# Graph network, four layers on one core: layer 3's early products in float32r halves, count matrices finished earlier, layer 4's loads moved

## The chip, the cores and the metric

The kernel runs on one core of one Trainium2 chip, in one launch. A core has a matrix engine (PE, with PEld for its weight loads), a vector engine (DVE), an activation engine (ACT), a general engine (POOL), a sequencer that here only issues transfers (SP), and 16 DMA engines. ACT, SP and POOL issue transfers from their own instruction streams. PE multiplies with a stationary operand of at most 128 x 128, sums in PSUM, eight banks of 128 x 512 float32. The metric is the time of one execution on the device, in microseconds (us); less is better.

## The reference

6250 nodes with 256 features, 100,000 edges sorted by their destination; half of all edges end at the first quarter of the nodes.

```python
h = relu(layernorm(x))
h = sage_mean(h)          # mean over in-edges of h[src]; h @ W_self + mean @ W_neigh + b
h = sage_pool(h)          # hp = relu(h @ W_pool + b_pool); max over in-edges of hp[src]
h = sage_gcn(h)           # (sum over in-edges of h[src] + h) / (deg + 1) @ W_neigh + b
h = sage_mean(h)
return x + (h @ W_fc + b_fc)
```

The hidden width is 512, the output width 256.

## The kernel before

Nodes are worked on in 49 row tiles of 128. The weights of layers 3 and 4 are multiplied together ahead, so layer 3 sums rows of 512 columns and layer 4 rows of 256.

**Sums.** A sum over in-edges is made in two ways. For the first tiles, where the edges are dense, a matrix of edge counts (128 source rows by 128 destination rows, kept in HBM as fp8 in `tab_a`) is multiplied with the table's rows: function `dense`, with `a` the counts as stationary operand and `z` a row tile as moving one. For the others the rows are gathered by edge (`sums`, POOL's `ring` gathers) and multiplied with 0/1 matrices. Layer 1 does so for 8 tiles densely, layer 3 for 18 (`H3`), layer 4 for 22 (`H4`). In layer 3 a float32 row is kept as three bf16 parts (`r3`, 3 x 512 columns in `tab_r`), so one row tile and one destination tile take three bf16 products. [...]

**The pooling layer** (L1650, from 732 to 1901 us). 782 steps of 128 edges: POOL gathers rows `X` (256 KB), DVE makes a running maximum with one and a half operations a step (L1631), SP stores the rows back two steps at a time (L1635). Six `X` tiles are in flight. Work of other layers is laid between the steps, by a counter `at`. `hub` builds the narrow count matrices (functions `build_narrow`, destination tiles 8 to 21, 448 rows `hm` and `ht`): 320 of them up to step `EARLY_AT` = 250 with `hm` made on DVE (L380), and 128 between steps 270 and 640 (`REST`) with `hm` made on ACT (L376 and L378). Row tiles finish in `done2` (one each 13 steps from step `FIRST_AT` = 112 on, when the block of edges that holds them is through; the carries between blocks are the products `ptcf`, `pcf`, and the last tile is `last_done2`). Source tiles 10 to 41 (`EARLY`) are taken for layer 3 as they finish: `early_products` makes batches of four, loads their counts for each of the 18 destination tiles on SP (`ae`, L1601), multiplies (L575) and adds into `acc3` on DVE (`add3`, L1307). `early.advance` spreads what is ready over at most 32 steps. The first 10 tiles' rows stay in SBUF (`kept_rows`) for layer 3; until those tiles finish, its places hold rows of the batches.

**Layer 3** multiplies what is left: the kept rows and tiles 42 to 48, which are read back into `zt` tiles (`resident`). Counts come through `stream`, four pieces ahead on ACT's queue (`ac`). `done3` finishes a tile and stores it.

**Layer 4** keeps some of layer 3's row tiles in SBUF (`z4_kept`, 23 tiles), reads the other 26 back (`z4_late`), and streams counts in the same way, cast three pieces ahead. `load4` loads a tile's input row `xr` and its own part `q` on ACT's queue (L1848, L1850, seven buffers each), DVE adds them (L1864), adds the scaled sum (L1866), and SP stores `out` (L1869). The order written is changed by a scheduler only through what the pools' buffers and the engines allow.

## Time and profile before

| | us |
|---|---|
| median of 3 runs | 2769.23 (2764.82 to 2772.06) |
| the profiled execution | 2768.88 |
| its span in the trace | 2767.1 |

| engine | busy us | share of the span |
|---|---|---|
| PE | 2363.3 | 85% |
| DVE | 2074.8 | 75% |
| POOL | 1881.4 | 68% |
| PEld | 1341.6 | 48% |
| ACT | 1240.6 | 45% |

The mean granted PE clock is 0.936 and the DMA engines move 295 GB/s in the mean. The shares are means over stages with different limits, so the stages are read apart: layer 1 up to 731 us, the pooling layer with its tail up to 1956, layer 3 up to 2390, layer 4 to the end. A row of the profile gives the line, the engine, the operation, what goes out and in, the count, the busy time and the mean ns of one; behind the second bar stands the idle time of the engine before these instructions, and what ended it. A chain is a path of waits followed back from the last instruction; its rows are a start, a duration and a place.

### The profile page before, as it was taken

To read this page: it belongs to the slowest core of one execution; us is meant where nothing else is said; L and a number is where in the kernel's file an instruction comes from. 1 tells how busy PE (TensorE), PEld (TensorE's weight loads), DVE (VectorE), ACT (ScalarE), POOL (GpSimd) and SP (SyncE) were. 2 spreads that over 40 slices of the span, in tenths; PEclk is the share of its full clock that TensorE was granted. 3 is DMA by queue.
4 is the path that set the end of the run, shared out by engine and by line. 5 is a ranking of instruction groups with operands and counts; after the bars stand their busy time and mean duration, and the time that the engine had idled before them with its cause. 6 is when DMAs were issued, how large, how long until landed. Compare 5 with 4: busy or idle time off the path is not lost.

```text
span 2767.1 us, 38367 instructions
## 1 busy us (share of the span) xinstructions
PE 2363.3 (85%) x10823; PEld 1341.6 (48%) x10913; DVE 2074.8 (75%) x5438; ACT 1240.6 (45%) x2833; POOL 1881.4 (68%) x2193
## 2 busy tenths in 40 slices
PE   3688999999686565788899998799899999798897
PEld 2356666767443222343344443344344444476676
DVE  8888777766699898788788897774376777466666
ACT  5467777763388887753444343211000000244333
POOL 5477777777566676777667776663477777577675
PEclk8799999999897687899999999999999999899999
DMA  8567777777799999999999999895799999999897
GB/s 273 154 183 204 208 210 212 223 228 222 243 362 334 309 351 318 331 347 345 315 307 331 342 357 298 296 311 189 280 370 382 379 391 388 328 344 308 284 302 225
DMA packets 360123, 815.18 MB, mean 295 GB/s; under 512 B 58798, under 2 KB 149014, under 8 KB 359868
## 3 DMA queue, kind: packets, MB, share of 16 engines
q0 software_dynamic: 145168, 511.30, 56.6%
q1 hardware_dynamic: 142248, 211.90, 21.1%
q10 hardware_dynamic: 72484, 89.43, 9.5%
q8 instruction: 89, 1.46, 0.2%
q14 instruction: 134, 1.10, 0.1%
HBM read 607.75 MB, written 205.46 MB: 294 GB/s over the span
## 4 chain that ended last, share of the span: by engine, by line
PE 45%; DMA 27%; DVE 14%; issue 5%; ACT 3%; POOL 2%; ACTq 0%; DVEq 0%; POOLq 0%
PE pd L575 14%; PE pg L516 11%; DMA X<-rows,srcIf 9%; DVE run L1631 5%; PE pd L569 4%; DMA ring<-tab_h,srcT 4%; DMA rows<-X 4%; PE pm_hp L1176 3%; DMA xr<-in_x 2%; DVE X L1631 2%; PE pm_prf L1548 2%; PE pm_hp L1170 2%; PE pb L346 2%; POOL X L1650 2%; DVE acc L547 1%
## 5 line engine op out<-in xcount | busy, mean ns | idle before, releaser
L1650 POOL DMA_INDIRECT X<-rows,srcIf x782 | 742.6, 950 | 346.6 <-issue 147.5
L1631 DVE SCALAR_TENSOR_TENSOR run<-run,samef,X 128x512 f32<-128x512 f32 x758 | 572.4, 755 | 65.3 <-DMA X<-rows,srcIf 59.6
L495 POOL DMA_INDIRECT ring<-tab_h,srcT x474 | 456.3, 963 | 148.9 <-issue 53.4
L516 PE MATMUL pg<-ring,hot 128*128 128x256 bf16 (+2 forms) x2342 | 492.1, 317 | 45.7 <-DMA ring<-tab_h,srcT 33.5
L575 PE MATMUL pd<-kept_rows,ae 128*128 128x512 bf16 x1520 | 395.0, 393 | 61.2 <-DVE acc L1307 48.2
L495 POOL DMA_INDIRECT ring<-tab_r,srcE x314 | 317.4, 1011 | 126.6 <-issue 49.4
L547 DVE SCALAR_TENSOR_TENSOR acc<-pg,M,acc 128x256 f32<-128x256 f32 (+2 forms) x629 | 322.8, 540 | 76.6 <-PE pg L516 72.5
L569 PE MATMUL pd<-zt,af 128*128 128x512 f32 x1078 | 305.8, 406 | 46.9 <-ACT af L1750 40.1
L516 PEld LDWEIGHTS <-hot 128*128 128x128 bf16 x2364 | 230.7, 98 | 233.2 <-issue 88.0
L495 POOL DMA_INDIRECT ring<-tab_s,srcE x266 | 254.4, 956 | 122.7 <-PE pg L513 48.7
L1631 DVE SCALAR_TENSOR_TENSOR X<-X,samef,run 128x512 f32<-128x512 f32 x379 | 282.2, 744 | 53.8 <-DMA X<-rows,srcIf 35.0
L575 PEld LDWEIGHTS <-ae 128*128 128x128 fp8e4 x1728 | 171.8, 100 | 305.3 <-issue 156.7
L569 PEld LDWEIGHTS pd<-zt,af 128*128 128x128 f32 x1078 | 208.0, 195 | 104.8 <-ACT af L1750 44.4
L1750 ACT CAST af<-ac 128x896 fp32r<-128x896 fp8e4 (+2 forms) x176 | 146.6, 846 | 217.5 <-PE pd L569 53.8
L491 DVE TENSOR_SCALAR hot<-iota_bf,keyE 128x128 bf16<-128x128 bf16 (+1 forms) x580 | 152.9, 284 | 107.8 <-PE pg L516 75.4
L1548 PE MATMUL pm_prf<-unf,hTf 128*128 128x512 f32 x384 | 197.4, 641 | 3.3 <-ACT hTf L1538 3.3
L401 ACT ACTIVATE A<-pb 128x392 fp8e4<-128x392 f32 x224 | 109.3, 499 | 191.2 <-PE pb L396 177.9
L338 ACT ACTIVATE hs<-ht,onef 128x128 bf16<-128x128 bf16 x396 | 153.5, 393 | 88.7 <-PE pb L346 87.7
L575 PE MATMUL pd<-Z,A 128*128 128x256 bf16 (+1 forms) x1176 | 184.6, 274 | 0.7 <-ACT A L351 0.6
L372 ACT ACTIVATE ht<-iota_bf,skR 128x128 bf16<-128x128 bf16 x448 | 155.9, 400 | 13.3 <-DMA col<-in_L_gnn_b 9.4
L337 ACT ACTIVATE ht<-iota_bf,sk 128x128 bf16<-128x128 bf16 x396 | 153.1, 398 | 8.3
L340 DVE TENSOR_SCALAR hm<-iota_w,mk 128x392 bf16<-128x392 f16 x461 | 150.5, 334 | 5.1 <-PE pb L346 4.8
(378 smaller groups left out, 3794.5 us busy)
## 6 DMA issues: line engine op xcount, KB each, us to landing
rows<-X SPq DMA_DIRECT2D x385, 256.0 KB
tab_r<-kept_rows ACTq DMA_DIRECT2D x44, 384.0 KB
ac<-tab_a ACTq DMA_DIRECT2D x128, 112.0 KB
rows<-hpf SPq DMA_DIRECT2D x49, 256.0 KB
th<-tab_t ACTq DMA_DIRECT2D x49, 256.0 KB
X<-rows,srcIf POOLq DMA_INDIRECT x782
tab_a<-A ACTq DMA_DIRECT2D x14, 784.0 KB
tab_t<-th SPq DMA_DIRECT2D x37, 256.0 KB
```

The source lines that it names most:

```text
L337: nc.scalar.activation(t, iota_b, AF.Abs, bias=sk[:, r : r + 1])
L338: nc.scalar.activation(hots[0], t, AF.Relu, bias=one, scale=-1.0)
L372: nc.scalar.activation(held["ht"][:, i, :], iota_b, AF.Abs, bias=sk[:, r : r + 1])
L491: nc.vector.tensor_scalar(hot[j], iota_b, keyT[:, j - jb : j - jb + 1], None, op0=ALU.is_equal)
L495: nc.gpsimd.indirect_dma_start(out=ring[:, j % deep, :].bitcast(F32) if wide else ring[:, j % deep, :], out_offset=None, in_=table, in_off ...
L516: mm = nc.tensor.matmul(pg[:, : F + c], hot[j], X[:, part * F : (part + 1) * F + c], start=(k == 0 and part == 2), stop=(k == n - 1 and pa ...
L547: nc.vector.scalar_tensor_tensor(acc[d], half, m, acc[d], op0=ALU.mult, op1=ALU.add)
L569: nc.tensor.matmul(hold[0], a, z, start=(s == ss[0]), stop=(s == ss[-1]))
L575: nc.tensor.matmul(hold[0][:, : F + c], a, z[:, part * F : (part + 1) * F + c], start=(s == ss[0] and part == 2 and s != own), stop=(s == ...
L1548: nc.tensor.matmul(pm, hT[:, c, :], un[:, c, :], start=False, stop=(c == KH - 1))
L1631: nc.vector.scalar_tensor_tensor(put, held, st, row, op0=ALU.mult, op1=ALU.max)
L1650: nc.gpsimd.indirect_dma_start(out=X[:, k, :], out_offset=None, in_=tab_p, in_offset=bass.IndirectOffsetOnAxis(ap=srcI[:, t : t + 1], axis=0),
```

## The change

(a) The early products take two float32r halves in place of three bf16 parts, for source tiles 8 to 39 in place of 10 to 41; the counts are cast on ACT (`aw`). `done2` makes the halves (two ACT copies and two products with `minus_r` and `ident_r`) ahead of the three parts, which still go to HBM. (b) All 448 narrow rows are built by step 310 with `hm` on DVE; early products begin behind step 320. (c) In layer 3 eight kept rows are halves, nine tiles are resident, and counts come in four pieces per tile. (d) In layer 4 twelve tiles are kept and 37 read back; counts are loaded nine pieces ahead, casts two ahead with four buffers; `load4` issues on SP.

```diff
-EARLY = (10, 42)
+EARLY = (8, 40)
-EARLY_AT = 250
-REST = (270, 640)
+EARLY_AT = 310
...
-                if late:
-                    t = pool.tile([P, NT * WIN2], BF16, name="hd", bufs=2)
-                    nc.scalar.activation(t, iota_w[:, : NT * WIN2], AF.Abs, bias=mk[:, r : r + 1],
-                                         scale=-1.0)
-                    nc.scalar.activation(hm, t, AF.Relu, bias=one, scale=-1.0)
-                else:
-                    nc.vector.tensor_scalar(hm, iota_w[:, : NT * WIN2], mk[:, r : r + 1], None,
-                                            op0=ALU.is_equal)
+                nc.vector.tensor_scalar(hm, iota_w[:, : NT * WIN2], mk[:, r : r + 1], None,
+                                        op0=ALU.is_equal)
...
-            for part in () if wide else (2, 0, 1):
+            order = () if wide else (1, 0) if s in halved else (2, 0, 1)
+            for part in order:
...
+            if d < EARLY[1]:
+                r2 = row_parts(d)
+                top_, rest_ = r2[:, :FH], r2[:, FH:]
+                nc.scalar.copy(top_, pm)
...
+                    nc.tensor.matmul(pm, minus_r, top_, start=False, stop=True, skip_group_check=True)
...
+                nc.scalar.copy(rest_, pm)
...
+                    nc.tensor.matmul(pm, ident_r, top_, start=False, stop=True, skip_group_check=True)
...
+        def widened(got):
+            if 1 not in got:
+                got[1] = early_pool[0].tile([P, BATCH, P], F32R, name="aw", bufs=4)
+                nc.scalar.copy(got[1], got[0])
...
-                    got[0] = early_pool[0].tile([P, BATCH, P], F8, name="ae", bufs=16)
+                    got[0] = early_pool[0].tile([P, BATCH, P], F8, name="ae", bufs=14)
...
+                    if i >= 2:
+                        widened(loaded[i - 2])
...
+                    if at == EARLY_AT + 8:
+                        while copies:
+                            copies.pop(0)()
+                        side.close()
+                        early_pool.append(side.enter_context(
+                            tc.tile_pool(name="early3", bufs=1, side="right")))
...
-                    early.advance(early.done + math.ceil(
-                        early.left() / max(1, min(32, T - 24 - at))))
+                    if at > EARLY_AT + 10:
+                        early.advance(early.done + math.ceil(
+                            early.left() / max(1, min(32, T - 24 - at))))
...
-            got[i] = pool.tile([P, 7, P], F8, name="ac", bufs=5)
+            got[i] = pool.tile([P, 7, P], F8, name="ac", bufs=deep + 1)
...
-                wide[i] = wide_pool.tile([P, 7, P], F32R, name="af", bufs=5)
+                wide[i] = wide_pool.tile([P, most_wide, P], F32R, name="af", bufs=4)
...
-        z4_kept = ((20, 27), (27, 34), (34, 41), (41, 43))
-        z4_late = ((0, 7), (7, 14), (14, 20), (43, NT))
+        z4_kept = ((31, 37), (37, 43))
+        z4_late = ((0, 7), (7, 14), (14, 20), (20, 26), (26, 31), (43, NT))
...
-            late = ((0, 5), (5, KEPT), (EARLY[1], NT))
+            late = ((0, 4), (4, KEPT), (EARLY[1], 45), (45, NT))
...
-                nc.scalar.dma_start(xr[:n, :], x[d * P : d * P + n, :])
+                nc.sync.dma_start(xr[:n, :], x[d * P : d * P + n, :])
...
-                nc.scalar.dma_start(q[:n, :], xq[d * P : d * P + n, :])
+                nc.sync.dma_start(q[:n, :], xq[d * P : d * P + n, :])
...
-                           wk)
+                           wk, deep=9)
```

DVE at the end of the pooling layer, before: `X2` and `run` are the pooling steps, `acc3` the sums of early products, `segf` and `cTf` the carry of block 1, which waits for PE's `ptcf`.

```order
L1631 SCALAR_TENSOR_TENSOR X2_21026<-run_20668,samef_140,X2_21026 128x512 [waits DMAHW3_49,DMASW5_49,DVE_49]
L1631 SCALAR_TENSOR_TENSOR X2_21026<-X2_21026,samef_140 128x512 [waits DMASW6_49,DVE_49]
L1307 TENSOR_TENSOR acc3_14_10829<-acc3_14_10829,pd_20618 128x512 [waits PE_49]
L1398 SCALAR_TENSOR_TENSOR segf_20726<-keepTf_10856,ptcf_20663 128x128 [waits PE_49]
L1398 SCALAR_TENSOR_TENSOR segf_20741<-keepTf_10856,ptcf_20663 128x128
...
L1307 TENSOR_TENSOR acc3_15_10830<-acc3_15_10830,pd_20659 128x512 [waits PE_49]
L1307 TENSOR_TENSOR acc3_16_10831<-acc3_16_10831,pd_20695 128x512 [waits PE_49]
L1307 TENSOR_TENSOR acc3_17_10832<-acc3_17_10832,pd_20752 128x512 [waits PE_49]
L1426 TENSOR_TENSOR fixf_20781<-fixf_20781,pcf_20815 128x512 [waits PE_49]
```

And with the change, the same place up to the end of the steps; `ptcf_20698` is block 0's own carry, which comes last.

```order
L1669 SCALAR_TENSOR_TENSOR run_20198<-run_20198,samef_144,X2_20548 128x512
L1306 TENSOR_TENSOR acc3_17_10835<-acc3_17_10835,pd_20539 128x512 [waits PE_49]
L1669 SCALAR_TENSOR_TENSOR run_20198<-run_20198,samef_144,X2_20561 128x512 [waits DMASW0_49,DVE_49]
...
L1669 SCALAR_TENSOR_TENSOR run_20198<-run_20198,samef_144,X2_20685 128x512
L1669 SCALAR_TENSOR_TENSOR X2_20692<-run_20198,samef_144,X2_20692 128x512 [waits DMAHW2_49,DMASW0_49,DVE_49]
L1669 SCALAR_TENSOR_TENSOR X2_20692<-X2_20692,samef_144 128x512 [waits DMASW1_49,DVE_49]
L1400 SCALAR_TENSOR_TENSOR segf_20706<-keepTf_10859,ptcf_20698 128x128 [waits PE_49]
L1400 SCALAR_TENSOR_TENSOR segf_20710<-keepTf_10859,ptcf_20698 128x128
L1404 TENSOR_TENSOR cTf_20705<-segf_20706,contTf_10860 128x128 [waits DVE_49]
L1404 TENSOR_TENSOR cTf_20705<-segf_20710,contTf_10860 128x128 [waits DVE_49]
```

The sums `acc3_15` to `acc3_17` and block 1's carry, which stood behind the last step, have moved ahead of it: the last sum has 37 rows of steps behind it, and the last step is followed by block 0's carry at once.

PE in one batch of early products, before: `pd` is the sum, `ae` the fp8 counts, each row tile taking three products with a weight load each (the rows in between are other tiles' work).

```order
L575 MATMUL pd_17459<-kept_rows_10833,ae_17290 128x512
L575 LDWEIGHTS ae_17290
L575 MATMUL pd_17459<-kept_rows_10833,ae_17290 128x512
L396 LDWEIGHTS hs_17082
L396 MATMUL pb_17502<-hm_16963,hs_17082 128x196 [waits PE_49]
L575 LDWEIGHTS ae_17290
L575 MATMUL pd_17459<-kept_rows_10833,ae_17290 128x512
L575 LDWEIGHTS ae_17290
L575 MATMUL pd_17459<-kept_rows_10833,ae_17290 128x512
L575 LDWEIGHTS ae_17290
L575 MATMUL pd_17459<-kept_rows_10833,ae_17290 128x512
```

And with the change, with `aw` the cast counts and `r2` the halves of a tile that is not kept (a weight load is not a row of its own here).

```order
L574 MATMUL pd_18806<-kept_rows_12092,aw_18758 128x512 x4
L574 MATMUL pd_18806<-r2_8_18001,aw_18758 128x512 x2
L574 MATMUL pd_18838<-kept_rows_12092,aw_18780 128x512 [waits DVE_49]
L574 MATMUL pd_18838<-kept_rows_12092,aw_18780 128x512
L1552 MATMUL pm_prf_18841<-usA_10852,th2_18724 128x512 [waits DMAHW2_49,Activation_49]
L1552 MATMUL pm_prf_18841<-usA_10852,th2_18724 128x512
L574 MATMUL pd_18838<-kept_rows_12092,aw_18780 128x512 x4
L1555 MATMUL pm_prf_18841<-usB_10853,th2_18724 128x512 x2
L574 MATMUL pd_18838<-r2_8_18001,aw_18780 128x512 x2
```

Each row tile takes two products where it took three, and other tiles' work still stands between them.

SP in the middle of layer 4, before: only output stores.

```order
L1869 DMA out_0<-xr4_26006 128x256 [waits DMAHW1_49,DVE_49]
L1869 DMA out_0<-xr4_25936 128x256 [waits DMAHW0_49,DVE_49]
L1869 DMA out_0<-xr4_26169 128x256 [waits DMAHW7_49,DVE_49]
L1869 DMA out_0<-xr4_26099 128x256 [waits DMAHW3_49,DVE_49]
L1869 DMA out_0<-xr4_26332 128x256 [waits DMAHW6_49,DVE_49]
L1869 DMA out_0<-xr4_26212 128x256 [waits DMAHW1_49,DVE_49]
L1869 DMA out_0<-xr4_26375 128x256 [waits DMAHW2_49,DVE_49]
L1869 DMA out_0<-xr4_26506 128x256 [waits DMAHW6_49,DVE_49]
```

And with the change, the same stores with the loads of `xr4` and `q4` (each `DMAHW` name is a lane of transfers whose landing is waited for).

```order
L1895 DMA q4_26269<-xq_70 128x256 [waits DMAHW2_49,DVE_49]
L1914 DMA out_0<-xr4_25350 128x256 [waits DMAHW4_49,DVE_49]
L1893 DMA xr4_25826<-in_x 128x256 [waits DMAHW6_49,DMAHW4_49]
L1914 DMA out_0<-xr4_25275 128x256 [waits DMAHW0_49,DVE_49]
L1893 DMA xr4_25842<-in_x 128x256 [waits DMAHW2_49,DMAHW0_49]
L1895 DMA q4_26324<-xq_70 128x256 [waits DMAHW3_49,DVE_49]
L1895 DMA q4_26388<-xq_70 128x256 [waits DMAHW5_49,DVE_49]
L1914 DMA out_0<-xr4_25509 128x256 [waits DMAHW2_49,DVE_49]
L1893 DMA xr4_25989<-in_x 128x256 [waits DMAHW4_49,DMAHW2_49]
L1914 DMA out_0<-xr4_25385 128x256 [waits DMAHW6_49,DVE_49]
```

The loads stand between the stores. The lane that a store takes is also waited for by the `xr4` load right behind it (`DMAHW4_49`, `DMAHW0_49`, `DMAHW2_49`, `DMAHW6_49`), and the `q4` loads wait for DVE.

More of the change, by code (lines that the diff above doesn't have):

```diff
@@ L557, in sums, with dense @@
         del todo[:]
-    def dense(ss, block, rows, F, psd, done, extra=0, wide=False, own=None):
+    def dense(ss, block, rows, F, psd, done, extra=0, wide=False, own=None, halved=()):
         hold = {}
@@ L1446, in row_parts @@
             i = d % ROWS3
+            assert early.done >= over.get(d + ROWS3, 0)
             if i < KEPT:
-                return kept_rows[:, i, :]
-            return early_pool[0].tile([P, 3 * FH], BF16, name=f"r3_{i}", bufs=1)
+                return kept_rows[0][:, i, :]
+            return early_pool[0].tile([P, 2 * FH], F32R, name=f"r2_{i}", bufs=1)
         def last_done2(d):
@@ L1623, in fast_path @@
         copies = []
-        first, rest = (
-            [w for d in ds for w in build_narrow(d, (skR, mkR, RB1), wk, banks, copies, d >= H3)]
-            for ds, banks in ((range(H1, H3), psb), (range(H3, H4), pst))
-        )
+        first = [w for d in range(H1, H4)
+                 for w in build_narrow(d, (skR, mkR, RB1), npool, psb, copies)]
         hub = Hub(first, 12)
-        more = Hub(rest, 12)
         def step(put, held, st, row):
@@ L1756, in stream @@
             widened(1)
-            widened(2)
         def block(d, s):
```

107 lines of the change are left out of this document (69 added, 38 removed).

## The prediction

> **What bounds the kernel now.** I read the busy time by stage first, to see which engine is near its limit in each stage that the change touches. The cuts are: 800 to 1085 us and 1200 to 1896 us (the pooling layer, before and after most count matrices are built), 1896 to 1956 (its tail), 1956 to 2390 (layer 3), 2390 to 2440 (start of layer 4), 2440 to 2767 (the rest of layer 4). The last three columns are the granted TensorE clock, the share of the DMA engines' time, and GB/s.
>
> ```profile
> core 0: us, PE busy (x) PEld busy (x) DVE busy (x) ACT busy (x) POOL busy (x), PEclk, DMA share, GB/s
> 800.00:1085.00 285.00, 185.18 (x601) 88.25 (x599) 262.41 (x713) 242.00 (x558) 197.53 (x208) 0.80 0.96 335
> ...
> 1200.00:1896.00 696.00, 618.78 (x2369) 287.75 (x2412) 571.30 (x841) 249.51 (x544) 472.01 (x499) 0.95 0.95 322
> 1896.00:1956.00 60.00, 56.93 (x193) 27.57 (x195) 17.40 (x50) 14.13 (x25) 4.07 (x5) 1.00 0.30 100
> 1956.00:2390.00 434.00, 414.52 (x1871) 187.59 (x1909) 299.45 (x693) 22.80 (x55) 319.18 (x316) 0.99 0.99 372
> 2390.00:2440.00 50.00, 35.01 (x133) 26.99 (x132) 12.68 (x40) 15.89 (x19) 30.05 (x33) 0.84 1.02 363
> 2440.00:2767.00 327.00, 291.36 (x1210) 230.51 (x1208) 205.21 (x633) 127.78 (x154) 222.53 (x233) 0.96 0.89 290
> ```
>
> Early in the pooling DVE is the bound (262 of 285 us). Later no engine is alone: PE 89%, DVE 82%, DMA 0.95. The tail is PE alone, with DMA at 0.30. Layer 3 has PE at 96% and DMA at 0.99 together. Layer 4 has PE at 89% with DMA at 0.89.
>
> Second, I read the pooling pace from the same windows, for the gather alone (each is one step of 128 edges, the number behind x):
>
> ```profile
> 1191.00:1896.00 705.00, 443.88 (x469) 0.95 0.95 323
> ...
> 1200.00:1240.00 40.00, 27.69 (x30) 1.00 0.98 347
> 1520.00:1560.00 40.00, 28.36 (x31) 0.96 0.99 342
> 1600.00:1640.00 40.00, 28.35 (x31) 1.00 0.99 345
> 1720.00:1760.00 40.00, 23.61 (x25) 1.00 0.88 281
> 1840.00:1880.00 40.00, 23.24 (x25) 0.93 0.88 281
> ```
>
> The late part makes a step in 705 / 469 = 1.503 us. Where the DMA share is 0.98 or more, it makes 30 to 31 steps in 40 us, about 1.31 us each; where the share falls to 0.88, it makes 25 (1.60 us) while PE has a full clock. So something other than DMA holds the slow stretches. Third, the waits there, of SP (which stores the rows and loads the early count blocks in one queue) and of the others, in us and times:
>
> ```profile
> SPq L1601 <- PE pd L575: 33.6, 33, 3.5
> ...
> POOL X L1650 <- DVE run L1631: 56.7, 78, 4.0
> DVE run L1631 <- DMA X<-rows,srcIf: 55.8, 42, 6.8
> ```
>
> SP stands 33.6 us behind early products before it may load the next count block, and the stores of pooled rows stand behind it.
>
> **The tail.** Fourth, the pooling's last operation on DVE (duration min/median/max in ns, then first and last start), and the chain of waits around it (start, us, what):
>
> ```profile
> L1631 DVE SCALAR_TENSOR_TENSOR X<-X,samef x1: 752/752/752, 1901.4 to 1901.4; 128x512 f32<-128x512 f32 x1
> ...
> 1902.30 0.44 PE ptcf L1385 x4
> ...
> 1941.74 0.44 PE pt_hTf L1469 x4
> 1942.18 0.45 PE ptcf L1385 x4
> ...
> 1953.33 0.59 ACT kept_rows L1499
> ...
> 1953.97 0.39 PE pm_last L1503
> ...
> 1956.84 20.18 DMA zt<-tab_r
> ```
>
> DVE's last pooling operation starts at 1901.4, yet block 0's carry products (ptcf) run on PE only at 1942.18: PE works off a backlog for 40 us. From there the last tile needs 14.7 us to 1956.84. In the changed order the sum of the last early product stands ahead of the last pooling steps on DVE, and after block 0's carry PE has some 28 rows, all of the last two tiles. So the 40 us go, and 5 us of backlog may stay. The last tile now makes f32r halves behind its three bf16 parts: two copies on ACT and three matmuls. One copy and one product of this kind take 0.59 and 0.39 us in these rows, so I put 3 us on it. Tail: -40 + 5 + 3, about **-30** (range -18 to -36).
>
> **The late pooling.** The groups that the change touches, with the mean ns of one:
>
> ```profile
> L575 PE MATMUL pd<-kept_rows,ae 128*128 128x512 bf16 x1520 | 395.0, 393 | 61.2 <-DVE acc L1307 48.2 <-ACT acc L1310 9.6 <-DMA rows<-X 0.9
> L569 PE MATMUL pd<-zt,af 128*128 128x512 f32 x1078 | 305.8, 406 | 46.9 <-ACT af L1750 40.1 <-DMA zt<-tab_s 6.7
> L569 PEld LDWEIGHTS pd<-zt,af 128*128 128x128 f32 x1078 | 208.0, 195 | 104.8 <-ACT af L1750 44.4 <-issue 14.4
> L575 PEld LDWEIGHTS <-ae 128*128 128x128 fp8e4 x1728 | 171.8, 100 | 305.3 <-issue 156.7 <-DMA rows<-X 1.8 <-DMA th<-tab_t 0.2
> ...
> 1863.78 2.10 PE L575 MATMUL pd<-kept_rows,ae 128*128 128x512 bf16 x9
> 2428.70 2.43 PE L569 MATMUL pd<-zt,af 128*128 128x512 f32 x10
> ...
> L575 PEld LDWEIGHTS <-ae 128*128 128x128 fp8e4 x1592 | 157.8, 100 | 277.6 <-issue 138.9 <-DMA rows<-X 1.8 <-DMA th<-tab_t 0.2
> ```
>
> Nine bf16 products in a row take 2.10 us, so one each (2.10 - 0.39) / 8 = 0.214 us; ten f32r products take 2.43, so (2.43 - 0.41) / 9 = 0.225 us. The new form costs the same per product, and there are 2 in place of 3. The last row is the window 1200 to 1896 alone: 1592 of the 1728 products lie in it. They leave (341 us), and all 1152 + 36 of the new kind come in (267 us), with two more products in each of some 33 row tiles that finish there (15 us): PE falls from 619 to about 560 us, 1.19 us a step against 1.32. The 128 late builds leave as well. PE is then no bound at 1.31 us a step, the pace at full DMA share; DVE, at 571 / 469 = 1.22 us of work a step, nearly is. SP's count loads wait for a cast on ACT, which is idle for two thirds of this stage, and no longer for PE. If all of it went to the pace of 1.31, 469 steps would save 90 us; if the X loop itself (gather, DVE, store) sets the slow stretches, 0. I take a little under half, **-40** (0 to -70), since the X loop's waits of 57 and 56 us remain.
>
> The Trainium skill, page "TensorE: Matmul & The Clock Gate", section on Fast Weight Load, says the fast load is for inputs that are not FP32, which speaks against float32r counts. The trace agrees on the load (195 against 100 ns) and shows that it is hidden behind the product before it; were the 95 ns not hidden, 1188 of them would be 113 us more on PE, 1.43 us a step, and the saving of this part could be 30 us at most, the sum below -19.
>
> **The early pooling.** All 448 narrow rows are built by step 310, where 320 were by step 250: 448 / 294 = 1.52 a step against 1.37. On DVE a comparison is
>
> ```profile
> L380 DVE TENSOR_SCALAR hm<-iota_w,mkR 128x196 bf16<-128x196 f16 x320 | 74.6, 281 | 19.5 <-PE pb L396 19.4
> L401 ACT ACTIVATE A<-pb 128x392 fp8e4<-128x392 f32 x224 | 109.3, 499 | 191.2 <-PE pb L396 177.9 <-DMA th<-tab_t 8.2 <-DMA rows<-X 4.5
> ```
>
> so 0.15 x 0.281 x 294 = 12 us more on the bound engine, if its own pace holds; ACT (85% busy) also gets a tenth more. Against it the early products no longer begin there, which takes PE work out. I take **+8** (0 to +30), and **+3** for the change of pools at step 318 (0 to +10), where the new products can begin only when the last copies of the builder have left.
>
> **Layer 3.** 8 kept rows for 18 destination tiles lose one product each: 144 x 0.214 = 31 us less PE. The DMA share is 0.99 and the bytes stay, so only a part shows: **-8** (0 to -25). The 36 casts go to ACT, busy 23 of 434 us.
>
> **Layer 4.** At its start 37 row tiles are read back in place of 26: 11 x 256 KB = 2.9 MB at the 363 GB/s of that stretch is **+8** (+3 to +12). Then comes the step I trust least. The xr and q loads move from ACT's queue to SP's, behind the output stores. With seven buffers each xr load waits until the store just ahead of it has landed. On ACT that wait held up casts; on SP it holds up the next store, and the q loads behind it wait for DVE's additions. The chain and waits of before:
>
> ```profile
> 2596.67 4.07 DMA out<-xr
> ...
> 2600.80 4.19 DMA xr<-in_x
> ...
> 2605.08 0.42 DVE xr L1864
> ...
> L1869 SPq DMA_DIRECT2D out<-xr x47: 298/332/914, 2449.5 to 2761.2; - x47
> ...
> DVE xr L1864 <- DMA xr<-in_x: 99.1, 27, 5.7
> PEld pd L569 <- ACT af L1750: 35.2, 22, 5.6
> PE pd L569 <- ACT af L1750: 25.9, 21, 5.1
> ```
>
> A store takes 4.13 us until the load behind it starts, the load 4.28 us until DVE adds. Today 46 intervals between stores fill 311.7 us: 13.55 us for a pair of tiles (one summed by gathers, one by count products). In the new order a pair is a ring: store, 4.13, load; trigger 0.33; second store, 4.13, load; 4.28; DVE's addition, then 7 to 11 DVE rows (0.324 us each, 205.21 / 633) to the next tile's finish: 2.3 to 3.6. Together 15.2 to 16.5 us, 1.6 to 2.9 us over today's pair; for 22 pairs +35 to +64. Against it: ACT is free of these waits, and PE's 36 us of idle in this stage, most of it waiting for casts (25.9 us, and 35.2 of its loads), is what counts nine pieces ahead could save at most. I take **+30** (-30 to +64), near the ring's lower end, since the trace shows both of its legs.
>
> The Trainium skill, page "DMA: Bandwidth & Descriptors", section "Anatomy of one DMA", gives about 2 us and the bytes at 436 GB/s; an estimate from it for 128 KB is 2.3 us, and a ring of 10 us. The trace has 4.07 and 4.19, so the rows decide; with the page's price the ring would bind nothing, and that is the second rival.
>
> **The sum.** -30 - 40 + 8 + 3 - 8 + 8 + 30 = -29 against the profiled execution's 2768.9 us (span 2767.1), which lies 0.4 below the median of 2769.2. Forecast: 2740 us.
>
> **Rivals.** (1) Slower: the ring on SP sets layer 4 at its full +64 and the pooling is held by its X loop, -15: -29 + 34 + 25 = +30, 2799 us. For it speak the DVE waits of 99.1 us for xr, against it that ACT no longer stalls. With the pooling at -15 it decides from 15.5 us a pair. Chance 0.12. (2) The ring does not bind, because its transfers land sooner or the stores come early; layer 4's loop is 0: 2710 us. For it: DMA is at 0.89 there, against it the two rows above. Chance 0.24. (3) The slow stretches of the pooling are the X loop's own, its gain 0, all else as forecast: 2780 us. For it: the 57 and 56 us of waits between X's gathers and DVE; against it SP's 33.6. Chance 0.16. (4) The f32r loads are not hidden among other products: 1188 x 0.195 = 232 us on PE, 792 us for 469 steps that take 705 today, so +87 in place of -40: -29 + 127 = +98, 2867 us; the row of ten speaks against it. Chance 0.02. (5) The ring at its full +64 gives back what pooling and tail save as forecast: -29 + 34 = +5, 2774 us, no change. Chance 0.06. The forecast's own case (2715 to 2765) has 0.40.
>
> **How the numbers follow.** About 0.3% (8 us) is what a measurement of this kernel can tell from no change: 2761 to 2777. Faster: rival 2 (0.24) and nearly all of the forecast's case (0.38): 0.62. Same: 0.02 of it, rival 5, and 0.07 of rival 3, whose 2780 lies at the edge: 0.15. Slower: rivals 1, 4 and the rest of 3: 0.23. The range runs from 2690 (rival 2 with the pooling at -60) to 2795, just short of rival 1's middle: it leaves out half of rival 1, rival 4, the lower part of rival 2 and some of the rest, about 2 in 10.
>
> **What would show it.** Right: block 0's ptcf within 10 us of the last pooling operation; under 1.45 us a gather from step 320 on; a PE product of `aw` 0.22 us behind the last; in layer 4 stores in pairs 15 to 16 us apart, with DVE's addition waiting for xr. Wrong: gathers still at 1.5 us with PE under 80%; an early part over 20 us longer; PE or DVE gaps in layer 4 that go, or that exceed 64 us in sum.

## The result and the profile after

The kernel is slower: 2785.8 us median (2779.1 to 2790.9) against 2769.5, ratio 1.0059 with the 95% interval 1.0034 to 1.0085. The forecast of 2740 us was wrong in its sign; the stated range, 2690 to 2795, still holds the result. The profiled execution has a span of 2777.2 us against 2767.1, so 10.1 us of the 16 can be looked for in the two traces. First the stages of the changed kernel (columns as before: PE, PEld, DVE, ACT, POOL, then the granted clock, the DMA share and GB/s), cut where its own stages end.

```profile
800.00:1085.00 285.00, 176.11 (x585) 84.80 (x584) 262.84 (x703) 246.47 (x568) 199.33 (x209) 0.77 0.95 333
...
1916.00:1940.00 24.00, 16.08 (x46) 7.91 (x47) 7.58 (x21) 4.93 (x9) 0.94 (x1) 0.77 0.45 141
1940.00:2362.00 422.00, 393.40 (x1710) 189.38 (x1745) 290.93 (x688) 41.89 (x85) 314.94 (x314) 0.98 1.00 380
2362.00:2420.00 58.00, 35.44 (x96) 24.63 (x94) 18.19 (x57) 11.99 (x15) 36.94 (x39) 0.74 0.93 341
2420.00:2777.00 357.00, 309.08 (x1252) 242.97 (x1250) 204.50 (x629) 137.17 (x163) 217.22 (x227) 0.94 0.85 270
```

The tail has shrunk from 60 us to 24, and layer 4 has lost DMA share (0.85 against 0.89). Cut at the first gathers of layers 3 and 4 in both kernels, layer 3 has some 16 us less PE (408 to 393) in nearly the same time. Where the stages begin and end is read from the first and last starts of the gathers (`X` in the pooling, `tab_r` in layer 3, `tab_s` in layer 4) and of the output stores, of before (first four rows) and after (last four):

```profile
L1650 POOL DMA_INDIRECT X<-rows,srcIf x782: 940/946/1386, 731.7 to 1895.4; - x196
L495 POOL DMA_INDIRECT ring<-tab_r,srcE x314: 940/946/1724, 1960.3 to 2373.3; - x157
L495 POOL DMA_INDIRECT ring<-tab_s,srcE x266: 940/946/1207, 2387.9 to 2750.8; - x133
L1869 SPq DMA_DIRECT2D out<-xr x49: 298/332/914, 2431.7 to 2761.2; - x49
```

```profile
L1688 POOL DMA_INDIRECT X<-rows,srcIf x782: 940/946/1462, 732.7 to 1914.0; - x196
L492 POOL DMA_INDIRECT ring<-tab_r,srcE x314: 942/946/1723, 1941.9 to 2354.6; - x157
L492 POOL DMA_INDIRECT ring<-tab_s,srcE x266: 940/946/1340, 2367.8 to 2759.6; - x133
L1914 SPq DMA_DIRECT2D out<-xr x49: 263/338/741, 2431.2 to 2770.5; - x49
```

| stretch | before | after | difference | forecast |
|---|---|---|---|---|
| start to the first pooling gather | 731.7 | 732.7 | +1.0 | 0 |
| first to last pooling gather | 1163.7 | 1181.3 | +17.6 | -29 |
| last gather to layer 3's first gather | 64.9 | 27.9 | -37.0 | -30 |
| to layer 4's first gather | 427.6 | 425.9 | -1.7 | -8 |
| to the first output store | 43.8 | 63.4 | +19.6 | +8 |
| to the end of the span | 335.4 | 346.0 | +10.6 | +30 |
| sum | 2767.1 | 2777.2 | +10.1 | -29 |

The forecast of the second row is +8, +3 and -40. Tail, layer 3 and layer 4 in sum (-8.5) came out near their forecast of 0, in part by luck, since the misses of the rows (-7, +6, +12 and -19) nearly cancel. The pooling did not: counted by gathers started, and read to about 1 us, its first 320 steps took 5 us longer, and steps 320 to 781 took 708.7 us against 696, where 656 had been forecast.

```profile
1199.00:1895.00 696.00, 618.78 (x2368) 287.73 (x2412) 572.23 (x843) 249.51 (x544) 472.01 (x499) 0.95 0.95 323
```

```profile
1205.00:1913.00 708.00, 618.41 (x2113) 380.08 (x2132) 590.27 (x907) 265.42 (x494) 475.05 (x503) 0.93 0.95 325
```

The first row is of before, the second of after, over the same steps: PE has the same 618 us of work in both, though 560 had been forecast, the share of DMA is the same, and PE's clock is a little lower. The loss does not lie evenly in these steps: steps 350 to 400 took 77.9 us against 67.1, steps 400 to 781 took 589.4 against 587.6. Steps 350 to 400 of before, then of after:

```profile
1241.00:1308.00 67.00, 54.70 (x209) 24.91 (x212) 59.80 (x86) 20.37 (x48) 50.02 (x54) 0.90 0.98 343
```

```profile
1247.00:1325.00 78.00, 59.42 (x194) 34.48 (x194) 55.85 (x89) 42.88 (x86) 51.11 (x55) 0.84 0.98 341
```

The DMA share is 0.98 in both, at nearly one rate: some 3.6 MB more (78 us at 341 GB/s against 67 at 343) took the 11 us.

### The profile page after: what moved, and what is told of

Same layout as the page of the kernel before. It is cut to its first block, busy times and chain, and to the rows that moved or that the text cites. A ratio compares the mean times of both kernels' runs of the same rounds, so it can differ in the third digit from the quotient of the medians.

```text
span 2777.2 us, 37443 instructions
## 1 busy us (share of the span) xinstructions
PE 2299.6 (83%) x10201; PEld 1418.2 (51%) x10256; DVE 2092.7 (75%) x5568; ACT 1287.6 (46%) x2837; POOL 1877.5 (68%) x2193
## 4 chain that ended last, share of the span: by engine, by line
PE 42%; DMA 32%; DVE 11%; issue 5%; ACT 4%; POOL 3%; ACTq 0%; SPq 0%; DVEq 0%; POOLq 0%
PE pd L574 13%; PE pg L513 9%; DMA X<-rows,srcIf 8%; DMA ring<-tab_r,srcE 5%; DMA ring<-tab_h,srcT 4%; DVE run L1669 3%; DMA out<-xr 3%; PE pm_hp L1175 3%; PE pm_prf L1558 2%; DMA xr<-in_x 2%; PE pm_w L277 2%; PE pm_hp L1169 2%; DMA rows<-X 2%; DMA zt<-tab_s 2%; PE pb L349 2%
## 5 line engine op out<-in xcount | busy, mean ns | idle before, releaser
L1794 ACT CAST af<-ac 128x768 fp32r<-128x768 fp8e4 (+3 forms) x212 | 171.0, 808 | 435.5 <-DMA ac<-tab_a 175.1
L513 PEld LDWEIGHTS <-hot 128*128 128x128 bf16 x2364 | 220.8, 98 | 261.2 <-issue 127.3
L574 PE MATMUL pd<-kept_rows,aw 128*128 128x512 f32 x828 | 259.6, 438 | 11.1 <-ACT aw L1624 5.6
L566 PEld LDWEIGHTS pd<-zt,af 128*128 128x128 f32 x1078 | 215.2, 201 | 86.8 <-ACT af L1794 23.9
L488 DVE TENSOR_SCALAR hot<-iota_bf,keyE 128x128 bf16<-128x128 bf16 (+1 forms) x580 | 147.2, 279 | 97.7 <-PE pg L513 52.0
L1558 PE MATMUL pm_prf<-unf,hTf 128*128 128x512 f32 x384 | 204.3, 659 | 1.9 <-ACT hTf L1548 1.3
L574 PEld LDWEIGHTS pd<-kept_rows,aw 128*128 128x128 f32 x828 | 157.7, 193 | 73.3 <-issue 29.8
L1624 ACT CAST aw<-ae 128x512 fp32r<-128x512 fp8e4 x144 | 89.3, 621 | 161.3 <-PE pd L574 142.8
L488 DVE TENSOR_SCALAR hot<-iota_bf,keyT 128x128 bf16<-128x128 bf16 x474 | 125.4, 274 | 39.5 <-PE pg L513 38.4
```

The source lines that it names most:

```text
L488: nc.vector.tensor_scalar(hot[j], iota_b, keyT[:, j - jb : j - jb + 1], None, op0=ALU.is_equal)
L513: mm = nc.tensor.matmul(pg[:, : F + c], hot[j], X[:, part * F : (part + 1) * F + c], start=(k == 0 and part == 2), stop=(k == n - 1 and pa ...
L566: nc.tensor.matmul(hold[0], a, z, start=(s == ss[0]), stop=(s == ss[-1]))
L574: nc.tensor.matmul(hold[0][:, : F + c], a, z[:, part * F : (part + 1) * F + c], start=(first and s != own), stop=(s == ss[-1] and part == ...
L1558: nc.tensor.matmul(pm, hT[:, c, :], un[:, c, :], start=False, stop=(c == KH - 1))
L1794: nc.scalar.copy(wide[i][:, :n, :], got[i][:, :n, :])
```

## The experiments

Each group ran on one chip, with the kernel before in the same rounds. The groups differ: before took 2763 and 2764 us in the second and third, as in the result, but 3186, 3152 and 3184 us in the first, fourth and fifth, where transfers are slower (272 to 280 GB/s in steps 320 to 781, against 325). The chips' numbers on record are 0, 11, 1, 8 and 1: the third and the fifth group have the same number, so it is not shown that the chip itself makes the difference. Below, a fast group is one with 2763 or 2764 us for before, a slow one the others. Ratios to before, and stretches within one group, are compared; where a stretch is held against another group, the text says so.

**Loads on ACT again, and the three other runs of the first group.** e1 is the changed kernel with

```diff
-                nc.sync.dma_start(xr[:n, :], x[d * P : d * P + n, :])
+                nc.scalar.dma_start(xr[:n, :], x[d * P : d * P + n, :])
```

and the same for `q`.

> The changed kernel with the xr and q loads of layer 4 back on ACT's queue, all else as changed. Theory (the ring on SP): the stretch from the first output store to the end, 346 us with the change and 318 before, comes back to 318 to 325, and the time to about 2760 us (2753 to 2766). Rival (what costs in layer 4 is the 11 tiles read back more, the shorter run of casts and the deeper loads on ACT): the stretch stays over 338 and the time over 2778 us.

Measured 1.0003 of before (0.9981 to 1.0025), with 353.4 us from the first store to the end. The 318 us that the theory gives for before is short: from the first store it is 335.4 us. Without the changed kernel in this group, this decides nothing; it is repeated below.

e2 multiplies one half only:

```diff
-            order = () if wide else (1, 0) if s in halved else (2, 0, 1)
+            order = () if wide else (0,) if once else (1, 0) if s in halved else (2, 0, 1)
...
-                             lambda v, d=d: summed.append((d, v)), own=d, halved=ss)
+                             lambda v, d=d: summed.append((d, v)), own=d, halved=ss, once=True)
```

> The changed kernel with only one of the two halves multiplied in the early products (the other half's products are left out): 594 products fewer, at 0.233 us each 138 us less PE between step 320 and the end of the pooling. Theory (PE bounds that stretch, since the work of the tail now lies in it): steps 350 to 782, 674 us with the change, shrink by 40 us or more, the time to 2745 us or less. Rival (gathers, DVE and row stores set their own pace): under 12 us less, the time over 2774 us.

Measured 0.9932 (0.9908 to 0.9956). Steps 320 to 781 took 812 us against 835 in e1, whose pooling is that of the changed kernel: 23 us less for some 138 us of PE work. Neither theory's number: PE holds a part of the pace, a sixth of what was taken away. In e4 of this group, whose pooling is that of before, the same steps took 809 us, so the change lost some 25 us here, and only 3 of them in steps 350 to 400.

e3 loads the early counts on ACT:

```diff
-                    nc.sync.dma_start(got[0][:, : len(ss), :].bitcast(BF16),
+                    nc.scalar.dma_start(got[0][:, : len(ss), :].bitcast(BF16),
```

> The changed kernel with the early count blocks loaded on ACT's queue, so that SP's row stores no longer stand behind a load that waits for a cast (98.9 us of such waits on SP with the change). Theory (these waits hold the pooling): steps 350 to 782 take 15 to 30 us less, the time 2756 to 2771 us. Rival (PE sets it, and SP's waits lie beside it): within 6 us of the changed kernel, 2780 to 2792 us; ACT has 144 triggers of 0.33 us more, which it has room for.

Measured 0.9956 (0.9929 to 0.9984), steps 320 to 781 in 837 us against 835. Steps 350 to 400 took 15 us less than in e1 (78.7 against 94.1), and the steps behind them 17 us more. In sum the waits of SP lie beside the work, as the rival has it; against e1 the whole time is not clearly different.

e4 is the kernel before with the two loads on SP, the edit of the change itself (`nc.scalar` to `nc.sync` in `load4`).

> The kernel before with only the xr and q loads of layer 4 moved to SP's queue. Theory (the ring on SP): +20 to +30 us, about 2795 us, with output stores in pairs 15 to 16 us apart. Rival (the ring costs only together with the later rows of the change): within 8 us of the kernel before, 2762 to 2778 us.

Measured 1.0019 (0.9990 to 1.0048), some 7 us, with an interval that holds 0 and 15: the theory's 20 to 30 are excluded in this group, and the rival fits.

**The changed kernel as a mark** (c0, no edit). The second group is fast, like that of the result.

> The changed kernel itself, as the mark for the other runs of this group, since a group's chip may differ from that of the result. All theories expect its first result again: 1.003 to 1.009 of the kernel before.

Measured 1.0059 (1.0046 to 1.0072), 2780.2 us: the result again.

**No read-back of 11 tiles** (e5).

```diff
+            Z4.update({s: Z4[s + 11] for s in range(20, 31)})
             for s0, s1 in z4_late:
-                Z4.update(resident(wk, tab_s, FO, s0, s1))
+                if s0 not in (20, 26):
+                    Z4.update(resident(wk, tab_s, FO, s0, s1))
```

> The changed kernel with row tiles 20 to 30 of layer 4 not read back (their products use other tiles' rows that are in SBUF, so the same work with wrong values): 2.9 MB less at the start of layer 4. Theory (the read-back shares the transfers with the gathers that are in flight, which is why the time from layer 4's first gather to its first output store grew from 43.8 to 63.4 us): 12 to 22 us less than the changed kernel, all of it before the first output store. Rival (the read-back runs at the full 363 to 380 GB/s): 8 us less or under. Second rival (the first stores are late because of the xr and q loads on SP's queue behind the read-back): under 3 us.

Measured 1.0048 (1.0032 to 1.0063), 2.5 us under the mark, the intervals overlapping. The first store came 49.3 us after layer 4's first gather in place of 65.8, as the theory said; but the rest took 361.2 us in place of 347.3, so the 12 to 22 us of the whole were missed. A gain at the start was taken back by what follows.

**One count block for all early products** (e7).

```diff
+        one_ae = []
...
-                    got[0] = early_pool[0].tile([P, BATCH, P], F8, name="ae", bufs=14)
-                    nc.sync.dma_start(got[0][:, : len(ss), :].bitcast(BF16),
-                                      tab_a[d, :, ss[0] : ss[-1] + 1, :])
+                    if not one_ae:
+                        one_ae.append(early_pool[0].tile([P, BATCH, P], F8, name="ae", bufs=1))
+                        nc.sync.dma_start(one_ae[0][:, :, :].bitcast(BF16), tab_a[0, :, 0:BATCH, :])
+                    got[0] = one_ae[0]
```

> The changed kernel with the 144 count blocks of the early products replaced by one block, loaded once and used for all (wrong counts, the same casts and products): 9.4 MB less traffic and no count loads between SP's row stores. Theory (the early products' bulk is set by PE, and their start by the burst of count loads): 5 to 15 us less than the changed kernel in steps 320 to 782, mostly in steps 350 to 400. Rival (transfers bound the whole stretch, DMA share 0.95): 28 us less or more, by 9.4 MB at 335 GB/s. Second rival (PE alone): under 4 us.

Measured 1.0046 (1.0028 to 1.0064), 4 us under the mark in the median; in the profile steps 320 to 781 took 696.7 us against 708.7, 9 of the 12 us in steps 350 to 400, as expected. Steps 350 to 400 took 68.4 us, near the 67.1 of before. There the changed kernel shows the burst of count loads with which the early products begin (waits between 1280 and 1325 us: the sum in us, times, the longest):

```profile
ACT aw L1624 <- DMA ae<-tab_a: 12.3, 2, 11.3
POOL X L1688 <- DMA rows<-X: 9.9, 4, 7.1
DVE run L1669 <- DMA X<-rows,srcIf: 9.6, 3, 7.4
```

A cast waits 11.3 us at once for its count block, and gathers and stores of `X` land late at the same time.

**Loads on ACT, beside the mark** (e8). The edit is that of e1.

> The changed kernel with layer 4's xr and q loads on ACT's queue, beside the changed kernel itself on the same chip. Theory (the ring of stores and loads on SP costs the 10.6 us by which the stretch from the first store to the end grew): 8 to 20 us less than the changed kernel. Rival (the ring runs beside PE's work and the stretch grew because fewer tiles are kept): within 4 us of the changed kernel, or up to 8 us more from casts that wait behind loads on ACT.

Measured 0.9993 (0.9980 to 1.0007), 2761.4 us: 19 us under the mark. The stretch from the first store to the end fell from 347.3 to 326.4 us. So where the loads are issued decides, and the theory holds in this group. What stands on SP is seen in the changed kernel's chain in layer 4 (start, us, what), and in SP's waits between 2420 and 2777:

```profile
2606.39 4.07 DMA out<-xr
2610.48 0.33 SPq L1893
...
2610.90 4.04 DMA out<-xr
...
2615.01 3.34 DMA xr<-in_x
...
2618.37 0.42 DVE xr L1909
```

```profile
SPq L1893 <- DMA out<-xr: 111.1, 38, 4.6
SPq L1914 <- DVE xr L1911: 66.5, 24, 8.4
SPq L1895 <- DVE hot L488: 60.0, 17, 5.2
```

A store, its landing, the load behind it, the second store, its landing, the second load, then DVE: the ring that the prediction drew, with 111 us of waits for landings. From a store to the second store behind it the median is 15.5 us, against 13.6 before; 15 to 16 had been named as the sign.

**A tile of its own for the result** (e9). The last operation of layer 4 writes to a new tile, so that a load of `xr` waits for DVE's reading and not for the store:

```diff
+                o = wk.tile([P, FO], F32, name="o4", bufs=6)
...
-                    nc.vector.scalar_tensor_tensor(xr[:n, :], acc[:n, c : c + FO],
+                    last = c + FO >= acc.shape[1]
+                    nc.vector.scalar_tensor_tensor((o if last else xr)[:n, :], acc[:n, c : c + FO],
...
-                nc.sync.dma_start(out[d * P : d * P + n, :], xr[:n, :])
+                nc.sync.dma_start(out[d * P : d * P + n, :], o[:n, :])
```

> The changed kernel with the result of layer 4 in a tile of its own (six buffers), so that a load of xr waits for DVE alone and no longer for the landing of the store ahead of it; loads and stores stay on SP's queue in the same order. Theory (the ring: it is the wait for a landing inside SP's queue that costs, not the queue): 18 to 32 us less than the changed kernel, 0.992 to 0.999 of the kernel before. Rival (it is SP's queue itself, full of waits for DVE, that delays the loads): under 8 us less.

Measured 0.9882 (0.9862 to 0.9902), 2733.0 us: 31 us under before and 47 to 49 under the changed kernel, more than expected. The stretch from the first store to the end fell from 347.3 to 303.5 us. The load now follows its store at once; SP's timeline, SP's waits and DVE's in layer 4 of this run:

```profile
2599.75 0.34 SPq L1916 DMA_DIRECT2D out<-o  x1
2600.14 0.42 SPq L1893 DMA_DIRECT2D xr<-in_x  x1
2604.55 0.34 SPq L1916 DMA_DIRECT2D out<-o  x1
2604.94 0.42 SPq L1893 DMA_DIRECT2D xr<-in_x  x1
```

```profile
SPq L1916 <- DVE o L1913: 115.5, 36, 9.0
...
DVE xr L1909 <- DMA xr<-in_x: 43.6, 29, 4.0
```

SP now waits mostly for DVE's results, and only 1.5 us in all for the landing of stores; 0.39 us lie between store and load, and DVE's wait for `xr` has gone from 91.2 us (85.1 in the mark) to 43.6. PE is busy 285 of 303 us there, against 298 of 347 in the mark.

e10 joins the edits of e9 and e5.

> The same with row tiles 20 to 30 not read back (other tiles' rows in their place, the same work with wrong values). Alone, this read-back changed the time by 2.5 us, though layer 4's first store came 16 us sooner. Theory (the ring swallowed that gain; without the ring the read-back costs what its start shows): 8 to 18 us less than the run before it. Rival (PE's work decides from there on, the read-back lies beside it): under 4 us.

Measured 0.9865 (0.9837 to 0.9892), 4 us under e9 in the median, with overlapping intervals. In the profiles layer 4 (first gather to the end) is 359.5 us against 369.5, so by these the read-back is worth 10 us once the ring is gone. The median alone would fit the rival, so the size stays open: some 4 us by the medians, 10 by the profiles.

**PE's work taken out.** e11 makes two products in place of eight (with `once` as in e2):

```diff
-            order = () if wide else (1, 0) if s in halved else (2, 0, 1)
+            order = () if wide else (0,) if once and s in (ss[0], ss[-1]) else () if once else (1, 0) if s in halved else (2, 0, 1)
```

> The changed kernel with two products in place of eight for each batch and destination tile of the early products (864 products left out, 0.233 us each: 201 us less PE between step 320 and the end of the pooling); loads, casts and DVE's sums stay. Theory (PE is what lengthens steps 320 to 781, 708.7 us with the change: the tail's 41 us of PE work now lies in them): down to 610 to 650 us. Rival (gathers, DVE and the transfers of counts set the pace, 696.7 us without count loads): 690 us or more.

Measured 0.9999 (0.9984 to 1.0013), 0.6% under the mark's ratio, some 17 us. Steps 320 to 781 took 690 us:

```profile
1199.00:1888.00 689.00, 438.71 (x1253) 217.96 (x1253) 584.89 (x906) 253.79 (x493) 475.06 (x503) 0.79 0.97 334
```

PE's work fell by 180 us, from 618 to 439, and the stretch by 19 (by some 17 against e9, which has the changed kernel's pooling in the same group), which is the rival's number. So PE's work is not what sets the pace of these steps: a tenth of what was taken away came back. The DMA share rose to 0.97, which is 668 of the 689 us.

**The same tile in the kernel before** (e12, the edit of e9).

> The kernel before with the same tile of its own for layer 4's result. Theory (before, the same wait for a landing stood in ACT's queue and cost a part of the 99.1 us in which DVE waited for xr): 4 to 15 us less than the kernel before. Rival (there PE and the casts decide): within 4 us.

Measured 0.9914 (0.9896 to 0.9932), 22 us under before, more than the theory's 4 to 15. So before had a ring as well, on ACT. Layer 4 is 359.4 us there, and 359.5 in e10: with the ring gone from both, by these profiles all that the change costs in layer 4 is the read-back.

**What sets the pooling's pace?** The fourth and fifth group are slow ones. e13 has seven `X` tiles in place of six, e14 five (2 buffers and `at // G2 % 5 in (1, 3)`):

```diff
-        xmore = late.enter_context(tc.tile_pool(name="xrows2", bufs=3))
+        xmore = late.enter_context(tc.tile_pool(name="xrows2", bufs=4))
...
-                X = (xmore if at // G2 % 2 else xpool).tile([P, G2, FH], F32, name="X2")
+                X = (xmore if at // G2 % 7 in (1, 3, 5, 6) else xpool).tile([P, G2, FH], F32, name="X2")
```

> The changed kernel with seven X tiles of two steps in flight in the pooling layer in place of six. Theory (the ring gather, DVE, store, gather holds the slow stretches): steps 320 to 781 go from 708.7 to 680 us or less, the early steps as well, the time 25 us or more under the changed kernel. Rival (the DMA engines' rate, 0.93 to 0.95 of their time, or DVE's own order): within 10 us of 708.7.

> The changed kernel with five X tiles in flight. Theory (the ring): steps 320 to 781 go from 708.7 to 760 us or more, as a pace set by the ring alone would grow by 6/5. Rival (the DMA rate or DVE): under 25 us more.

Measured 0.9996 (0.9970 to 1.0023) and 1.0056 (1.0021 to 1.0090); steps 320 to 781 in 823 and 830 us. Six tiles were not run in this group; in e1, where before took 1% longer, they took 835. Seven against five are 7 us apart, where the theory had some 80, and e15, with seven as well, took 830. The number of tiles does not set the pace in a slow group.

e15 joins the edits of e13 and e9.

> The changed kernel with seven X tiles and with layer 4's result in a tile of its own: the sum of what the two brought alone, if they lie in different stages: 45 to 50 us less than the changed kernel from the second (0.988 of the kernel before), and with the ring theory another 25 us or more (0.980 or less); with the rival 0.985 to 0.990.

Measured 0.9979 (0.9950 to 1.0007), which fits neither number. Once more, in the fifth group, as e17:

> Seven X tiles and layer 4's result in a tile of its own once more, since the chip of the first run moved its transfers more slowly. If the ring of X tiles binds nothing, as that chip showed, 0.986 to 0.990 of the kernel before, as with the own tile alone (0.988); if it binds on a faster chip, 0.982 or less.

Measured 1.0001 (0.9976 to 1.0026). In these groups layer 4 from the first store on takes 349 and 351 us with the own tile and 352 without (e13), so taking the ring away changes nothing there, and the gain of 1.2% was found in the fast group alone.

e16 stores half of the columns of the pooled rows (zeros are put into the other half at the start, not shown here):

```diff
-                runs[b][r0 * P : (r0 + n) * P, :].rearrange("(g p) f -> p g f", p=P), rows)
+                runs[b][r0 * P : (r0 + n) * P, : FH // 2].rearrange("(g p) f -> p g f", p=P),
+                rows[:, :, : FH // 2])
```

> The changed kernel with only the left 256 of 512 columns of the pooled rows stored (the right half of the rows is filled with zeros at the start of the kernel, which makes the early part longer; only the steps are compared): 64 KB less per step of some 490 KB that the DMA engines move. Theory (the rate of the transfers sets the pace): steps 320 to 781 go from 708.7 to 620 to 660 us, in the ratio of the bytes. Rival (latencies in the X loop and DVE's order): 690 us or more.

Measured 837 us for steps 320 to 781, against 845 in e17 of the same group, which has seven tiles in place of six, with the DMA share down from 0.83 to 0.77: in a slow group the pace does not follow the bytes stored. The numbers of theory and rival had been set for a fast group, where this was not run. (The whole took 1.0477 of before; the pooling's first gather starts 145 us later than in e17, behind the zeros.)

e18 joins the edits of e16, e7 and e11.

> The changed kernel with half of the row stores, all count loads but one and 864 of the early products left out together. Theory (the transfers set the pace, PE holds a little of it): steps 320 to 781 in 560 to 620 us, where DVE, with some 1.22 us of work a step, becomes the bound (565 us). Rival (latencies in the X loop): 660 us or more.

Measured 803 us for these steps (the whole 1.0351 of before, with the zeros): 42 us under e17, still over the rival's 660, which was set for a fast group. Half of the row stores, all count loads but one and most early products together are worth 5% there.

## Why the prediction was wrong

**The late pooling (-40, measured +13)** is the step that failed, and it failed twice. First, PE's work did not fall to 560 us. The early products went as forecast: counted so that no stretch of PE's time counts twice, they fell by 78 us, from 360 to 283, where 74 (341 less 267) had been forecast, and f32r products start 0.23 us apart, near the 0.225 (four in a row):

```profile
1612.37 1.08 PE L574 MATMUL pd<-kept_rows,aw 128*128 128x512 f32 x4
1613.30 1.09 PE L574 MATMUL pd<-r,aw 128*128 128x512 f32 x4
1614.22 1.10 PE L574 MATMUL pd<-kept_rows,aw 128*128 128x512 f32 x4
```

But the tail's backlog was taken out of the tail and not put anywhere. Most of it was not early products but the finish of row tiles. One of its products, in steps 320 to 781 of before, in the tail of before, and in the steps of after (its tail has none):

```profile
L1548 PE MATMUL pm_prf<-unf,hTf 128*128 128x512 f32 x240 | 114.5, 603 | 0.0
L1548 PE MATMUL pm_prf<-unf,hTf 128*128 128x512 f32 x40 | 18.3, 592 | 0.0
L1558 PE MATMUL pm_prf<-unf,hTf 128*128 128x512 f32 x296 | 148.2, 629 | 0.3
```

All 40 of the tail now lie in the steps, and some 14 that ran ahead of step 320. In sum the finish of row tiles, without the new halves, rose there from 242 to 303 us, for which the forecast had nothing; the halves brought 20 us, where 15 had been forecast. So the 618 us stayed.

Second, PE's work was not the price: e11 took 180 us from PE and gained 19. The slow stretches at DMA shares of 0.88 were read as "something other than DMA", and PE, busy at 89%, was taken for it. What the step mis-sized is the transfers' own time. Its pace of 1.31 us a step was read from stretches in which a step moved 441 to 463 KB (30 or 31 steps in 40 us at 342 to 347 GB/s); the mean of these steps is some 487. The prediction's row of before has a DMA share of 0.95 over 696 us, which is 661 us of transfers (an estimate from that row) and more than the 656 forecast, and the bytes did not fall: 225 MB before, 230 with the change, from rate and length of the two rows. With the change it is 0.95 of 708, 673 us, and in e11 668 of 689. Rival 3 (no gain in the pooling, 2780 us, 0.16) came nearest in its number; that the X loop itself is the cause, as it says, is not shown. The +13 is for the most part the burst of count loads with which the early products now begin: 11 us in steps 350 to 400, which went when the loads were taken out (e7). In the slow group the loss in these steps, some 25 us, lay elsewhere, and its cause is open.

**The tail (-30, measured -37)** was right in its mechanism, and its chain now runs as drawn:

```profile
1919.18 0.76 DVE X L1669
...
1920.08 1.10 PE ptcf L1387 x4
...
1938.85 2.33 DMA tab_r<-r
...
1941.95 1.01 POOL ring L492
```

PE takes up block 0's carry 0.14 us after DVE's last pooling operation, where it was 40 us late. There was no backlog of 5 us.

**The early part (+11, measured +5) and layer 3 (-8, measured -2)** lay in their ranges; layer 3 has the DMA share at 1.00 and PE's 16 us less gave nearly nothing.

**Layer 4 (+38, measured +30)** was right in sum, and its two stretches missed in opposite ways: the first store came 20 us later, not 8 (16 of them are the read-back's, by e5), and the rest grew by 10.6 us, not 30. That these cancel in the table is luck. But e5 shows that the two are one: a later first store is caught up in a stretch that the ring bounds. The ring itself was larger than the difference of the two kernels shows, since before had one too: taking it away is worth 44 us of the stretch with the change and 21 before. The difference of the two, 23 us, and the read-back's 10 come to 33, near the +30, and near the forecast's own terms of 30 and 8: the mechanism was the one forecast.

**Weight loads (rival 4)** of 193 ns stayed hidden behind the products, as the row of ten had shown. Rival 2, a ring that binds nothing, came out wrong where the result was taken: stores landed 4.07 and 4.04 us after issue, and taking the ring away gained (e8, e9). In the slow groups taking it away gained nothing (e15 and e17 against e13). The Trainium skill's 2.3 us (an estimate from its page "DMA: Bandwidth & Descriptors", section "Anatomy of one DMA") does not agree with these rows; that section gives its fit for transfers issued by GpSimd, and these are issued by SP.

**Open** is what sets 1.5 us a step. In the fast groups it is not PE. The transfers are near their limit there (0.95 to 0.97 of the time), yet e7 took 9.4 MB out and gained 12 us, not the 28 of their rate; half of the row stores were taken out in a slow group alone. In the slow groups it is not the number of tiles nor the bytes stored. The waits of POOL for DVE and of DVE for gathers remain in every run, but no run took the gathers' own rate or DVE's work apart.

The version with its own tile for layer 4's result is the fastest of those that leave no work out, in a fast group: 0.988 of before. In the slow groups it was run only with seven `X` tiles, and equals before.

## What to carry to other kernels

When work that was late at the end of a stage disappears from there, ask into which stretch it went, and add it to the sum there before that stretch is called lighter. A busy share of 89% is no proof that an engine sets the pace: its work has to be taken away to know. Before a stretch is forecast shorter, hold the forecast against the busy share of the transfers times the stretch's length. A load that reuses the place of a result that is still being stored ties queue, landing and load into a ring; a tile of its own for the result costs a few buffers and cuts it, and it may pay in the kernel before as well.

## What the runs showed of the hardware

With 180 us less of PE work in the same stretch, the granted clock of PE fell from 0.93 to 0.79. The stages of the changed kernel go the same way: 0.77 where PE is busy 62% of the time (800 to 1085 us), 0.94 at 87% (from 2420 us on), 0.98 at 93% (1940 to 2362 us). Whether this takes back a part of what less PE work would gain is not shown.

The same program takes 14 to 15% longer in three of the five groups. The steps 320 to 781 of e17, in the columns as above:

```profile
1425.00:2262.00 837.00, 647.45 (x2115) 392.51 (x2134) 588.31 (x906) 269.65 (x502) 469.71 (x497) 0.88 0.83 272
```

The DMA engines moved 272 GB/s there at a share of 0.83, against 325 at 0.95 in the result, and the gain of the own tile was not there in the slow groups. For the loads on ACT only runs of different slow groups can be held together: 353 us from the first store to the end with them (e1), 352 with the loads on SP (e13).
